# Deformable convolution, attention and experts on one core: all eight chunks of batch 0 transposed on TensorE, and a gate on the finishing chains

## The chip, the core and the metric

The program runs on one core of a Trainium2 chip. The metric is the device time of one execution in microseconds (us), as a median over runs. The five engines each work through their own instruction list in the order in which the program wrote it: TensorE (PE; PEld is its weight load), VectorE (DVE), ScalarE (ACT), GpSimd (POOL) and SyncE (SP). SP here only issues transfers; an issue that waits holds up the issues written behind it.

## The reference, cut to what matters

The input is 4 images of 128 channels by 64 x 64 positions. Per image:

```python
x = x + deform_conv(group_norm(x))       # 3x3 taps: bilinear samples at learned offsets, times a mask,
                                         # then out[o, p] = sum over c, k of samples[c, k, p] * w[o, c, k]
t = to_tokens(x)                         # 4096 tokens of 128 features, 16 heads of 8
t = t + attn(ln(t))                      # q = k = v = ring of cosines; softmax(q q' / sqrt 8) q;
                                         # output projection, ln, feed forward (8 -> 512 -> 128), ln
t = t + experts(ln(t))                   # router over 8 experts, the best two weighted
```

Attention runs over all 4096 tokens of an image, so every token needs the keys of all others.

## The kernel before

**Chunks.** An image is cut into 8 chunks of 512 positions. `prepare(b)` makes everything that attention needs of image b: group norm, a table of corner values in DRAM, offsets and weights, and then `deform` and `convolved` chunk by chunk, which end in `features`: queries, keys and values of the chunk, written to DRAM.

**A chunk's sampling.** `deform` handles 12 units a chunk (3 groups of 3 taps, 4 blocks of 128 positions). A unit is three indirect gathers on POOL (line 625), one multiplication by the bilinear weights and two additions on DVE (lines 645, 650, 651). Then the samples must be turned from position-major to channel-major for the convolution. There are two ways:
- In order: TensorE transposes the unit's three 128 x 128 tiles into PSUM (line 662) and DVE copies them (line 665) into `sT`, which stays in SBUF. `sT` has one buffer, so a chunk's first unit waits until the convolution of the chunk before has read it (`summed`).
- By way of DRAM: DVE transposes 32 x 32 blocks (line 686, three instructions a unit), SP writes them to `smd` (line 698, 12 issues a chunk), and `convolved` reads them back into `sT` (line 731, 12 issues a chunk).

Before the change chunks 0 and 1 of image 0 go in order and the other 30 chunks by way of DRAM. `gather` keeps gathers up to four units ahead for the first 36 units of image 0, two units ahead otherwise; for the deeper lead it borrows spare buffers of another tag (`spare`, tag `et`).

`convolved` (line 281 is its helper `by_columns`) multiplies 9 taps, adds bias and residual (line 758), transposes (765) and runs `features`: layer norm, cosines and their products on DVE, one power (396) and one copy (823) on POOL, a transpose (836), and `hiT` and `loT` (838, 839), which SP writes to DRAM. A chunk counts as prepared some planned microseconds after that.

**Attention.** A step is one 128-token slice of keys against one chunk of queries, for the 4 heads of a group. `scores` issues 4 matmuls (1261) and 2 exponentials on ACT of 128 x 1024 elements each (line 1270), `context` 4 matmuls with the values (1281). There are 7400 exponentials in the program. While image 0 is being prepared, the runs are ordered so that they use what is there: exponentials 1 to 32 need chunk 0 alone, up to 128 chunks 0 and 1, up to 208 chunks 0 to 2, up to 512 chunks 0 to 3, up to 576 also chunks 4 and 5; after that all eight are needed. Runs over part of the keys park sums in DRAM (`part`, line 1126) and load them again (line 1456).

**Finishing.** When the four head groups of a chunk are done, `park_context` puts the chunk on the list `done`. Up to two chains `finishing` run: each takes a chunk from the list and runs `finish`, which loads the chunk's data (lines 1086 to 1102), then `attention_out` (transfers, projection 281 into `ao_ps`, layer norm), `feed_forward` (`z_ps`, `h_ps`, `f_ps`, layer norm) and `experts` (router, then eight expert matmul groups into `e_ps`, sums on DVE 1065 to 1075), ending in a transposed copy `y` (line 892) and the store (line 1081).

**What sets the order.** `Beside` is a planner that runs while the program is being written. It keeps planned times, and after each attention step it lets waiting jobs issue pieces of `prepare`, of finishing, and of other side work, within a budget of TensorE time per step. Each `yield need(...)` names the planned cost of a piece and the earliest planned time. `force` issues pieces of `prepare` without regard to the budget when attention has no keys to go on with; `drain` issues everything that is left after the last attention step, job by job. So the order on each engine is fixed when the program is built; on the chip nothing is reordered.

Of the kernel before, what the change touches and what calls it, by code (L numbers as in the profile page):

```python
# [202 lines left out]
def need(pe=0.0, dve=0.0, lat=0.0, hold=False, after=0.0):  # L203

    return pe, dve, lat, hold, after


def ve(n, ops=1):  # L210

    return ops * (0.17 + n / 960.0)
# [6 lines left out]
def tr(n):  # L219

    return 0.13 + 0.115 * n
# [3 lines left out]
def kernel(  # L225
# [47 lines left out]
    def misc(name):  # L273
        if alone:
            return ps_s.tile([P, 2, 512], F32, tag="sc", name=name)[:, 0, :]
        return ps_m.tile([P, 512], F32, tag="misc", name=name)
# [127 lines left out]
    def settle():  # L404

        nc.vector.tensor_reduce(is_hi, pick[:, 0], AX.XY, ALU.add)
        nc.vector.tensor_reduce(is_lo, pick[:, 1], AX.XY, ALU.add)
        nc.vector.tensor_copy(w1_h, w1_4)
        nc.vector.tensor_tensor(w1_4, w1_4, w1_h.bitcast(F32), ALU.subtract)
        nc.vector.tensor_scalar(w1_h, w1_h.bitcast(F32), is_hi, None, ALU.mult)  # L410
        nc.vector.scalar_tensor_tensor(w1_x, w1_4, is_lo, w1_h.bitcast(F32), ALU.mult, ALU.add)
        for _ in cosine(cry, ry_sb, cry_n, cry_r, 0.0):
            pass
# [185 lines left out]
    def deform(b, tab, idx, wt, rest):  # L599
# [7 lines left out]

        def early(n):

            return b == 0 and n < 3 * 12  # L610

        def gather(last):

# [20 lines left out]
        for n, (ch, kg, j) in enumerate(units):  # L634
            progress[b] = 0.1 + 0.9 * n / len(units)
            if b == 0 and n == 36:
                yield need(dve=5.0)
                settle()
            while not ahead:
                yield need(lat=0.5)  # L640
            v, landed = ahead.pop(0)
            v4 = v.rearrange("p k (q c) -> p (k q) c", c=C)
            w12 = wt[:, j, 3 * kg : 3 * kg + 3, :].rearrange("p k q -> p (k q)")
            yield need(dve=ve(1536), after=landed)
            nc.vector.tensor_tensor(v4, v4, w12[:, :, None].to_broadcast([P, 12, C]), ALU.mult)  # L645
            if moved:
                yield need(pe=0.01, dve=ve(384))
                moved.pop()()
            yield need(dve=ve(768) + ve(384))
            nc.vector.tensor_tensor(v[:, :, : 2 * C], v[:, :, : 2 * C], v[:, :, 2 * C :], ALU.add)  # L650
            nc.vector.tensor_tensor(v[:, :, :C], v[:, :, :C], v[:, :, C : 2 * C], ALU.add)  # L651
            if b == 0 and ch < 2:


                if n % 12 == 0:
                    while len(summed) < ch:
                        yield need(lat=0.5)
                    sT = big.tile([P, KK, CH], F32, tag="xs", name=f"sT_first{ch}")
                yield need(pe=tr(3), lat=FREE, hold=True)
                pt = misc(f"sT_ps{j}_{kg}")  # L660
                for k in range(3):
                    nc.tensor.transpose(pt[:, P * k : P * (k + 1)], v[:, k, :C], ident)

                def move(sT=sT, kg=kg, i=j % 4, pt=pt):
                    nc.vector.tensor_copy(
                        sT[:, 3 * kg : 3 * kg + 3, P * i : P * (i + 1)],
                        pt[:, : 3 * P].rearrange("p (k c) -> p k c", c=P),
                    )

                moved.append(move)  # L670
                beside.later(beside.now + 0.8, lambda n=n: gather(n))
                if n % 12 == 11:
                    yield need(pe=0.01, dve=ve(384))
                    moved.pop()()
                    featuring.append(True)
                    beside.add("prepare", convolved(b, ch, sT), 0.5, True)
                    if ch == 0:
                        yield from rest
                continue

            yield need(dve=ve(384))
            if j % 4 == 0:
                beside.flush(sent)
                tr9 = work.tile([P, 4, 4, 4, 32], F32, tag="st", name=f"tr{b}_{ch}_{kg}", bufs=NST)
            for k in range(3):
                nc.vector.transpose(  # L686
                    out=tr9[:, k, :, j % 4, :],
                    in_=v[:, k, :C].rearrange("p (c i) -> p c i", i=32),
                )
            beside.later(beside.dve, lambda n=n: gather(n))  # L690
            if j % 4 < 3:
                continue
            while kg == 0 and len(featuring) > 1:
                yield need(lat=1.0)

            def put(ch=ch, kg=kg, tr9=tr9):
                for o in range(4):
                    nc.sync.dma_start(
                        out=smd[ch % 2][:, 3 * kg : 3 * kg + 3, :, o].rearrange(
                            "i k c n -> i (k c) n"  # L700
                        ),
                        in_=tr9[32 * o : 32 * (o + 1), :3].rearrange("p k c j t -> p (k c) (j t)"),
                    )

            sent = beside.dve
            beside.later(sent, put)
            if kg == 2:

                while len(summed) < ch if b == 0 else featuring:
                    yield need(lat=1.0)  # L710
                featuring.append(True)
                beside.later(
                    beside.dve + 0.1,
                    lambda ch=ch: beside.add("prepare", convolved(b, ch), 0.5, True),
                )
# [163 lines left out]
    def bc4(v):  # L879
        return v[:, None, :].to_broadcast([P, 4, C])  # L880
# [14 lines left out]
    def attention_out(b, ch, r, aT, a4):  # L895


        yield need(dve=ve(512))
        nc.vector.tensor_tensor(r, r, bc4(b_comb), ALU.add)
        yield need(dve=ve(512), lat=0.2)  # L900
        nc.vector.tensor_tensor(aT, aT, a4.rearrange("p i c -> p (i c)"), ALU.mult)
        for i in range(4):
            if i % 2 == 0:
                yield need(pe=2 * MM128, dve=ve(512) if i else 0.0, lat=0.0 if i else FREE, hold=not i)
            if i == 0:
                po = misc(f"ao_ps{b}_{ch}")
            by_columns(
                po[:, C * i : C * (i + 1)], aT[:, P * i : P * (i + 1)], wcomb_sb, True, True
            )
        nc.vector.tensor_tensor(r, r, po.rearrange("p (i c) -> p i c", c=C), ALU.add)  # L910
        m = work.tile([P, 4], F32, tag="ln_m", name=f"m1{b}_{ch}")
        rs = work.tile([P, 4], F32, tag="ln_r", name=f"r1{b}_{ch}")
        yield from layer_norm_stats(r, m, rs, "ln")
        yield need(dve=ve(128, 4))
        normalized(a4, r, m, rs)
        yield need(dve=ve(512, 2), lat=0.2)
        nc.vector.tensor_tensor(a4, a4, bc4(g1), ALU.mult)
        nc.vector.tensor_tensor(a4, a4, bc4(beta1), ALU.add)
# [165 lines left out]
    def finish(b, ch):  # L1084
        x4 = temp2(f"x4_{b}_{ch}")
        nc.sync.dma_start(out=x4, in_=x2d[b][ch])

        rows = atd[b][ch].rearrange("g (h d) n -> (g h) d n", d=32)
        aT = temp2(f"aT{b}_{ch}", (P, CH))
        nc.sync.dma_start(out=aT, in_=rows[:, :HD])  # L1090
        rd = work.tile([P, CH // HD], F32, tag="rd", name=f"rd{b}_{ch}")
        nc.sync.dma_start(out=rd, in_=rows[:, HD].rearrange("h (q n) -> h q n", q=HD))
        r = temp2(f"r{b}_{ch}")
        nc.sync.dma_start(out=r, in_=xtd[b][ch])
        yield need(lat=4.0)
        yield need(dve=0.6, lat=0.1)
        nc.vector.reciprocal(rd, rd)
        yield need(lat=3.5)
        nc.sync.dma_start(out=rdd[b][ch].rearrange("h q n -> (h q) n"), in_=rd)
        yield need(lat=6.0)  # L1100
        a4 = temp2(f"a4_{b}_{ch}")
        nc.sync.dma_start(
            out=a4.rearrange("p i c -> p (i c)"),
            in_=rdd[b][ch].rearrange("h q n -> h (q n)")[:, None, :].to_broadcast([HEADS, HD, CH]),
        )
        yield from attention_out(b, ch, r, aT, a4)
        yield from feed_forward(b, ch, x4, a4)
        yield from experts(b, ch, x4)


    def park_context(b, g, sc, cu):
# [112 lines left out]

    landing = {}
    fetched = {}
    groups, done, active = {}, [], []

    def finishing():

# [125 lines left out]
    for n, (run, t) in enumerate(steps):  # L1356
        b, g, sc = runs[run][:3]
# [50 lines left out]
    n = issued = begun = 0  # L1408
    beside.rate = 1.0
    with tc.manual_schedule(engines={PE, DVE, SP, POOL}):  # L1410
# [6 lines left out]
        while n < len(steps):  # L1417
# [11 lines left out]
            b, g, sc, ts, kind = runs[run]  # L1429
# [145 lines left out]
```

## Time and profile before

| | before |
|---|---|
| median of 11 runs | 7461.85 us (7451.89 to 7480.11) |
| profiled execution: time, span | 7461.57 us, 7459.8 us |
| granted TensorE clock | 0.969 |
| PE busy | 7025.7 us (94%) |
| ACT busy | 6853.4 us (92%), of it 6839.4 in 7400 exponentials |
| DVE busy | 4464.3 us (60%) |
| POOL busy | 1659.7 us (22%) |
| first exponential starts, last ends | 174.0 us, about 7375 us |

The span runs from the first to the last instruction. Matmuls are pipelined, and a busy TensorE is not one at its peak. A group's line gives busy time, mean duration and the idle time of its engine before it with what ended that.

### The profile page before, as it was taken

To read this page: it belongs to the slowest core of one execution; us is meant where nothing else is said; L and a number is where in the kernel's file an instruction comes from. 1 tells how busy PE (TensorE), PEld (TensorE's weight loads), DVE (VectorE), ACT (ScalarE), POOL (GpSimd) and SP (SyncE) were. 2 spreads that over 40 slices of the span, in tenths; PEclk is the share of its full clock that TensorE was granted. 3 is DMA by queue.
4 is the path that set the end of the run, shared out by engine and by line. 5 is a ranking of instruction groups with operands and counts; after the bars stand their busy time and mean duration, and the time that the engine had idled before them with its cause. 6 is when DMAs were issued, how large, how long until landed. Compare 5 with 4: busy or idle time off the path is not lost.

```text
span 7459.8 us, 180754 instructions
## 1 busy us (share of the span) xinstructions
PE 7025.7 (94%) x73848; PEld 2352.9 (32%) x73848; DVE 4464.3 (60%) x8950; ACT 6853.4 (92%) x7467; POOL 1659.7 (22%) x1326
## 2 busy tenths in 40 slices
PE   3689999899999999999999999989999999999997
PEld 2222232223333333333333333323333333333333
DVE  7766366676445777775544778775444554455544
ACT  0579999899999999999999999989999999999995
POOL 5545044443001433431000434430000000000000
PEclk6889999999999999999999999999999999999998
DMA  6777477988446888887555888996454466666651
GB/s 182 225 211 232 132 243 245 306 258 279 146 165 228 292 270 274 280 277 231 201 180 195 266 287 293 313 314 225 172 180 150 158 234 232 237 223 229 233 194 64
DMA packets 909789, 1689.53 MB, mean 226 GB/s; under 512 B 150754, under 2 KB 384124, under 8 KB 858268
## 3 DMA queue, kind: packets, MB, share of 16 engines
q1 hardware_dynamic: 809102, 1371.37, 55.4%
q0 software_dynamic: 92160, 302.06, 12.4%
q8 instruction: 580, 9.50, 0.5%
q10 hardware_dynamic: 7694, 4.52, 0.2%
q14 instruction: 253, 2.07, 0.1%
HBM read 1027.51 MB, written 650.14 MB: 225 GB/s over the span
## 4 chain that ended last, share of the span: by engine, by line
PE 79%; DMA 10%; DVE 4%; issue 1%; SPq 1%; POOL 1%; ACT 1%; POOLq 0%; DVEq 0%; ACTq 0%
PE acc L1281 39%; PE sc L1261 23%; PE acc L1214 5%; PE e_ps L281 4%; PE conv_ps L281 3%; DMA et<-etd 3%; PE f_ps L281 2%; DMA etd<-st 1%; DMA sT<-smd 1%; PE om_ps L533 1%; DMA smd<-tr 1%; DMA v<-tab,idx 1%; DVE v L645 1%; DVE st L1140 1%; ACT e L1270 1%
## 5 line engine op out<-in xcount | busy, mean ns | idle before, releaser
L1270 ACT ACTIVATE e<-sc 128x1024 f32<-128x1024 f32 x7400 | 6839.4, 1084 | 414.9 <-PE sc L1261 331.5
L1281 PE MATMUL acc<-e,qf 128*9 128x512 f32 (+1 forms) x29600 | 3900.8, 599 | 12.1 <-ACT cu L1491 6.4
L1261 PE MATMUL sc<-qT,kT 32*128 32x512 f32 x14800 | 2323.7, 498 | 112.3 <-ACT e L1270 60.8
L1261 PEld LDWEIGHTS sc<-qT,kT 32*128 32x128 f32 x14800 | 925.6, 183 | 3533.8 <-ACT e L1270 3329.9
L625 POOL DMA_INDIRECT v<-tab,idx x1152 | 1459.6, 1267 | 1502.0 <-DVE tr L686 874.1
L1140 DVE STREAM_TRANSPOSE st<-e 128x1024 f32<-128x1024 f32 x792 | 937.4, 1222 | 714.7 <-ACT e L1270 606.1
L1281 PEld LDWEIGHTS acc<-e,qf 128*9 128x9 f32 (+1 forms) x29600 | 677.7, 91 | 580.4 <-issue 316.6
L396 POOL TENSOR_TENSOR r<-ln_t,expo 128x4 f32<-128x4 f32 x96 | 112.2, 1169 | 3097.3 <-DVE ln_t L394 3049.4
L645 DVE TENSOR_TENSOR v<-v,wt 128x1536 f32<-128x1536 f32 x384 | 667.3, 1738 | 129.7 <-DMA v<-tab,idx 128.0
L1214 PE MATMUL acc<-et,qv 128*9 128x128 f32 x12672 | 502.7, 277 | 72.6 <-DMA et<-etd 72.6
L1065 DVE TENSOR_TENSOR eo<-e_ps,gt 128x512 f32<-128x512 f32 x256 | 175.1, 686 | 534.5 <-PE e_ps L281 530.7
L650 DVE TENSOR_TENSOR v<-v 128x768 f32<-128x768 f32 x384 | 367.1, 956 | 10.1
L281 PE MATMUL conv_ps<-sT,wconv_sb 128*32 128x256 f32 x4320 | 348.5, 397 | 11.3 <-DMA sT<-smd 8.9
L1214 PEld LDWEIGHTS acc<-et,qv 128*9 128x9 f32 x12672 | 269.3, 90 | 272.1 <-issue 202.9
L686 DVE STREAM_TRANSPOSE tr<-v 128x128 f32<-128x128 f32 x1080 | 249.5, 282 | 52.0 <-DMA etd<-st 43.3
L1493 DVE COPY cu<-acc 128x512 f32<-128x512 f32 x116 | 80.2, 692 | 282.2 <-PE acc L1281 282.0
L651 DVE TENSOR_TENSOR v<-v 128x384 f32<-128x384 f32 x384 | 215.8, 562 | 13.3
L396 POOL TENSOR_TENSOR rstd<-lt_t,expo 128x4 f32<-128x4 f32 x32 | 56.5, 1766 | 542.0 <-DVE lt_t L394 519.3
L281 PE MATMUL f_ps<-w_sb,h 128*32 128x128 f32 x4096 | 166.5, 283 | 0.0
L950 DVE TENSOR_SCALAR h<-h_ps,b_sb 128x512 f32<-128x512 f32 x128 | 94.9, 743 | 99.5 <-PE h_ps L948 92.0
L823 POOL COPY fx<-rn 128x512 f32<-128x512 f32 x32 | 26.8, 839 | 521.6 <-DVE rn L822 303.2
L965 DVE TENSOR_TENSOR a<-a,f_ps 128x512 f32<-128x512 f32 x32 | 21.9, 685 | 196.2 <-PE f_ps L281 196.2
(227 smaller groups left out, 3164.8 us busy)
## 6 DMA issues: line engine op xcount, KB each, us to landing
etd<-st SPq DMA_DIRECT2D x396, 1024.0 KB
et<-etd SPq DMA_DIRECT2D x396, 1024.0 KB
kT<-kTd SPq DMA_DIRECT2D x372, 256.0 KB
smd<-tr SPq DMA_DIRECT2D x360, 192.0 KB
sT<-smd SPq DMA_DIRECT2D x360, 192.0 KB
qT<-qTd SPq DMA_DIRECT2D x166, 256.0 KB
atd<-cu SPq DMA_DIRECT2D x128, 256.0 KB
qf<-fqd SPq DMA_DIRECT2D x372, 72.0 KB
```

What stands on the lines that cost most here:

```text
L281: nc.tensor.matmul(dst[c : c + 32], lhsT=lhsT[:, c : c + 32], rhs=rhs, start=start, stop=stop)
L625: nc.gpsimd.indirect_dma_start(out=v[:, k, :], out_offset=None, in_=tab, in_offset=bass.IndirectOffsetOnAxis(ap=idx[:, j, kk : kk + 1], ax ...
L645: nc.vector.tensor_tensor(v4, v4, w12[:, :, None].to_broadcast([P, 12, C]), ALU.mult)
L650: nc.vector.tensor_tensor(v[:, :, : 2 * C], v[:, :, : 2 * C], v[:, :, 2 * C :], ALU.add)
L651: nc.vector.tensor_tensor(v[:, :, :C], v[:, :, :C], v[:, :, C : 2 * C], ALU.add)
L686: nc.vector.transpose(out=tr9[:, k, :, j % 4, :], in_=v[:, k, :C].rearrange("p (c i) -> p c i", i=32),)
L1065: nc.vector.tensor_tensor(ws[hf], pe.rearrange("p (e c) -> p e c", c=C), gt[:, i, 4 * hf : 4 * (hf + 1), None].to_broadcast([P, 4, C]), AL ...
L1140: nc.vector.transpose(out=st[:, :, 2 * pr : 2 * pr + 2, :].rearrange("p o h (q j) -> p o (h q) j", j=32), in_=es[pr].rearrange("p h (q o i ...
L1214: nc.tensor.matmul(acc[32 * h : 32 * h + QW, P * kt : P * (kt + 1)], lhsT=qv[:, at : at + QW], rhs=e[:, :, h, 32 * t : 32 * (t + 1)], star ...
L1261: nc.tensor.matmul(ps[i // 2][:, i % 2, :], lhsT=kT[h : h + 32, P * (t % 4) : P * (t % 4 + 1)], rhs=qT[h : h + 32, :], start=True, stop=True,)
L1270: nc.scalar.activation(e, ps[pr], AF.Exp, scale=1.0 / math.sqrt(HD))
L1281: nc.tensor.matmul(acc[32 * h : 32 * h + width, :], lhsT=flat[:, first : first + width], rhs=es[h // 2][:, h % 2, :], start=(t == ts[0]), ...
```

## The change

Three edits:
- `early(n)` holds for all units of image 0, so gathers run up to four units ahead there and two of five units sit in spare buffers.
- In `deform`, all eight chunks of image 0 take the in-order way; the way through `smd` remains for images 1 to 3.
- In `finish`, a list `heavy` is a gate between `attention_out` and `feed_forward`: a chain waits, one planned microsecond at a time, until no other chain is inside `feed_forward` or `experts`. It holds for every chunk of all four images.

```diff
         def early(n):
-            return b == 0 and n < 3 * 12
+            return b == 0
...
-            if b == 0 and ch < 2:
+            if b == 0:
                 if n % 12 == 0:
                     while len(summed) < ch:
                         yield need(lat=0.5)
                     sT = big.tile([P, KK, CH], F32, tag="xs", name=f"sT_first{ch}")
...
         yield from attention_out(b, ch, r, aT, a4)
+        while heavy:
+            yield need(lat=1.0)
+        heavy.append(True)
         yield from feed_forward(b, ch, x4, a4)
         yield from experts(b, ch, x4)
+        heavy.pop()
...
-    groups, done, active = {}, [], []
+    groups, done, active, heavy = {}, [], [], []
```

## The prediction

> **What bounds the kernel now.** I read the head of the page first, then busy time by stretches, then the costliest groups of the long stretch, then the timeline of ScalarE at the beginning and of all engines at the end.
>
> The stretches (us, then busy time of each engine with its count, granted clock, share of the DMA engines, GB/s):
>
> ```profile
> 150.00:600.00 450.00, 321.99 (x2514) 95.14 (x2514) 315.39 (x562) 287.41 (x320) 252.38 (x190) 0.82 0.75 229
> 600.00:850.00 250.00, 248.18 (x2078) 71.52 (x2076) 136.19 (x272) 249.63 (x273) 77.06 (x60) 1.00 0.58 172
> 5150.00:7375.00 2225.00, 2222.20 (x25075) 769.86 (x25076) 1063.06 (x2466) 2222.51 (x2429) 54.24 (x53) 1.00 0.58 199
> 7375.00:7459.80 84.80, 34.69 (x433) 21.17 (x425) 52.08 (x147) 0.23 (x1) 3.02 (x3) 0.64 0.07 23
> ```
>
> From 5150 to 7375 us ScalarE is busy for 2222.5 of 2225 us, and its group there was idle for 2.0 us:
>
> ```profile
> L1270 ACT ACTIVATE e<-sc 128x1024 f32<-128x1024 f32 x2411 | 2223.0, 1081 | 2.0 <-ACT e L1270 0.8 <-PE sc L1261 0.3 <-PE h_ps L948 0.2
> ```
>
> 2223.0 / 2411 = 0.922 us an exponential, back to back. ScalarE is the bound wherever attention has keys: finishing work written beside attention is free there, and taking it away gains nothing. Time is lost where ScalarE idles: before the first exponential (174 us), between first and last (by the stretches: 600 - 174 - 287.4 = 138.6 us up to 600, 0.4 to 850, 26.1 to 1150, 181 in the later preparations, about 350 in all), and after the last (85 us). The change acts on the first 900 us and on the end.
>
> ScalarE early on and around the last wait for keys:
>
> ```profile
> 218.02 0.59 ACT L1491 COPY cu<-acc 128x512 f32<-128x512 f32 x1 [1.22 <-PE acc L1281]
> 266.23 5.61 ACT L1270 ACTIVATE e<-sc 128x1024 f32<-128x1024 f32 x6 [47.62 <-PE sc L1261]
> ...
> 851.25 16.61 ACT L1270 ACTIVATE e<-sc 128x1024 f32<-128x1024 f32 x18 [0.26 <-PE sc L1261]
> 879.85 3.77 ACT L1270 ACTIVATE e<-sc 128x1024 f32<-128x1024 f32 x4 [11.99 <-PE sc L1261]
> ```
>
> 47.6 us wait for chunk 1, which was in order already, and 12.0 us for chunk 7. And the end, one finishing chain alone:
>
> ```profile
> 7375.89 0.69 DVE L1493 COPY cu<-acc 128x512 f32<-128x512 f32 x1
> ...
> 7386.78 0.69 DVE L892 COPY y_6T<-y_ps 128x512 f32<-128x512 f32 x1 [0.57 <-PE y_ps L890]
> 7387.39 0.54 DVE L1097 RECIPROCAL rd<-rd 128x64 f32<-128x64 f32 x1
> ...
> 7399.64 1.12 DVE L788 TENSOR_SCALAR a<-r,m,r 128x128 f32<-128x128 f32 x4 [1.19 <-POOL r L396]
> ...
> 7430.16 0.29 DVE L1007 COPY lT<-l_ps 128x128 f32<-128x128 f32 x1 [0.78 <-PE l_ps L1002]
> ...
> 7455.46 0.69 DVE L892 COPY y_7T<-y_ps 128x512 f32<-128x512 f32 x1 [0.57 <-PE y_ps L890]
> 7456.18 0.34 SPq L1081 DMA_DIRECT2D out_dram<-y_7T  x1
> ```
>
> A whole chain takes 7456.15 - 7387.47 = 68.7 us from one y to the next, every step waiting for the one before; the last store takes 3.65 us more.
>
> **Part 1, the gate: the end.** The order of instructions of both programs is fixed and can be compared. After the last scores, the order before holds the last part of chunk 6's experts and all of chunk 7. The changed order holds six outputs: chunk 2 from its router on (lT), chunks 4, 5, 6, 7 whole, and chunk 3 from the normalisation ahead of its feed forward. The cause is visible in the order: before, two chains alternate; now `z` transposes of successive chunks stand 168 exponentials (168 x 0.922 = 155 us) apart, one chain at a time. In batch 3 this falls behind. On DVE each whole finish stands strictly behind the y of the one before, so chains cannot overlap. Sum from the last context copy (ends 7376.58): chunk 2, 7430.16 to 7456.15, 26.0; four whole, 4 x 68.7 = 274.7; chunk 3, 7399.64 to 7456.15, 56.5; store 3.65. Together 360.9 against 7459.8 - 7376.6 = 83.2 now: **+278**. Attention returns nothing for it, for ScalarE idles 2.5 us in 5150 to 7375. Bounds: -15 if loads of the next chunk hide a little, +25 if each chain pays 5 us more at the lower clock (0.60 in this stretch): 263 to 303.
>
> The chain holds a write and a read back of the reciprocals: issue at 7387.96, read issued at 7389.73, consumer at 7392.93, so 1.8 and 3.2 us. The Trainium skill, "DMA: Bandwidth & Descriptors", in "Anatomy of one DMA — SWDGE (gpsimd) path", gives about 2 us fixed for a DMA, most of it the receipt of the write; these two are issued by SP. By it the two would be some 4 us instead of 5, an estimate, and the four whole chains 4 us shorter; I use the measured chain.
>
> **Part 2, a new wait at exponential 584.** Order before: chunk 7's transpose of `features` (836) stands behind exponential 564, 20 ahead of need. Changed: after exponential 584 stand the last two units' transposes, chunk 7's whole convolution (72 fours of matmuls in a row), line 765 and 836, and only then the next scores. Why so late: outside the opening runs the planner pays TensorE work from a budget, and the transposes (0.475 planned a unit, 5.7 a chunk) now come out of it. Queued behind the wait is all of attention. Chain by rows: multiplication, additions, transposes and copy of the last units about 8 us; convolution 9.8 (chunk 0, 114.2 to 124.0); 2.1 to the end of line 758; 29.5 from there to the end of `loT` (126.1 to 155.6); then 18.4 (chunk 0, 155.6 to 174.0) to 31 us (chunk 7, 849.0 to 879.9) until the next exponential. That is 68 to 81, less 2 for the exponential still running, less the 12 idle now: **+60** (54 to 67).
>
> **Part 3, the rest of the opening.** For chunks 2 to 7 of image 0 the change removes per unit 3 block transposes (3 x 0.282 = 0.85 us DVE) and adds one copy (0.55): 72 x 0.30 = 21 us less DVE. It adds 216 transposes on PE: in the trace 0.272 us in `fT_ps` at a granted clock of 1.00 and a median of 0.421 in `sT_ps` at 0.53 to 0.64, so 59 to 91 us of PE, beside ScalarE from 600 on. They are written between attention's own matmuls, so a late unit now holds attention, which the DVE route could not do. DVE waited 67.1 us for gathered samples from 174 to 900, 28 times; with a lead of four that shrinks, and 2.4 us a time is about what three score tiles hide: I take +15 (0 to 60).
>
> The Trainium skill, "TensorE: Matmul & The Clock Gate", Part 4, says that a transpose does not count as work that lifts the clock. The row above fits, 0.421 in the starved stretch. If all 216 ran so, TensorE would pay 91 us instead of 59, a difference of 32 us, an estimate that lies mostly under waits; the sum above does not use it.
>
> SP loses 24 issues a chunk, 144 in all. This is the gain:
>
> ```profile
> ACT cu L1491 <- PE acc L281: 49.6, 11, 12.0
> ```
>
> ScalarE waited 49.6 us, 11 times, for accumulators whose parked sums come late; in the SP list the load of `part` stood behind the `smd` and `sT` issues (8 of them from 269.4 to 275.8 just ahead of the 12.0 us wait). Between nothing and all 49.6 I take **-35**, as most lie next to such issues, some behind issues that wait for POOL.
>
> The order also moves the starving: chunk 2's features come after exponential 128 instead of 94, all that two chunks allow, so attention waits there; chunk 3's come after 176 instead of 200, against a need at 208, where ScalarE now idles 15.0 and 9.0 us (its timeline, at 482.6 and 499.9). Features of chunk 1 no longer stand behind chunk 2's units on DVE. I set these against each other: 0 (-20 to +25).
>
> **Batches 1 to 3.** 181 us of ScalarE idle time; the changed order holds about as many finishes in those stretches. I take 0, bounds -50 to +25.
>
> **Sum.** 278 + 60 + 15 - 35 + 0 + 0 = +318 on the profiled 7461.57 us (span 7459.8, 1.8 around it; the median of the runs is 7461.85): 7780.
>
> **Rivals.**
> - *POOL becomes the opening's limit.* Its list is in order; with four units ahead up to 2 x 3 x 1.27 = 7.6 us more gathers stand ahead of each power (396) and copy (823). Against: POOL is busy 252 of 450 us. Price: 2 x 7.6 a chunk, five chunks, +76: 7856. Chance 0.08.
> - *The tail overlaps after all.* DVE is busy 41.1 of the 68.7 us of a chain. If chains ran at DVE's pace, 4.8 of them (four, and 56.5 / 68.7) would save 27.6 each, 132: 7648. Against: DVE's own list puts them end to end. Chance 0.05.
> - *Faster: idle time inside attention is what the change returns.* Place: between first and last exponential, 350 us less the 47.6 that stay = 302. If the `smd` traffic and the second chain caused all of it, the wait at 584 included, 7461.6 + 278 - 302 = 7437. It decides only if over 92% of that idle time goes (278 / 302). For it: SP waits for DVE in the preparations. Against: 181 us lie in images that keep `smd`. Chance 0.01.
> - *The gate does nothing*, if chains rarely met: 7462 + 40 = 7502. The order speaks against it. Chance 0.01.
>
> **How the numbers follow.** The forecast has 0.85. Low ends: 263 + 54 + 0 - 50 - 20 - 50 = +197, high ends: 303 + 67 + 60 + 0 + 25 + 25 = +480; not all at once, so I take 7690 to 7870, which includes the POOL case. A difference under 0.2% (15 us) cannot be told from none. Faster 0.01, same 0.01, slower 0.98.
>
> **What would show it.** A stretch after the last exponential near 360 us with DVE about 60% busy and six y copies, four of them 68 to 70 us apart; one gap of ScalarE of 65 to 80 us ahead of exponential 585; waits for `acc L281` well under 49.6. If the tail stays under 150 us, or the last exponential ends before 7375, the prediction is wrong.

## The result and the profile after

The changed kernel takes 7790.6 us, median of 8 runs (7777.0 to 7799.3), against 7463.6 us for the kernel before (31 runs): a ratio of 1.0437 [1.0427, 1.0446], 4.4% slower. The forecast was 7780. The profiled execution has a span of 7790.1 us, 330.3 more than the 7459.8 before.

The stretches of the changed kernel, cut as before (us, then busy time of PE, PEld, DVE, ACT and POOL with counts, granted clock, share of the DMA engines, GB/s; the last two cuts are moved to its own last exponential):

```profile
150.00:600.00 450.00, 366.28 (x2907) 116.45 (x2907) 285.69 (x446) 326.60 (x363) 234.70 (x181) 0.87 0.60 188
600.00:850.00 250.00, 240.12 (x2015) 73.01 (x2014) 132.75 (x205) 228.75 (x248) 82.30 (x67) 0.98 0.43 136
5150.00:7428.00 2278.00, 2274.43 (x24953) 776.78 (x24945) 1020.53 (x2267) 2276.77 (x2490) 47.58 (x47) 1.00 0.59 202
7428.00:7790.10 362.10, 150.91 (x1778) 88.22 (x1778) 223.09 (x672) 4.36 (x10) 16.10 (x16) 0.62 0.06 18
```

Up to 600 us ScalarE does more than before (326.6 us against 287.4), up to 850 less (228.8 against 249.6). The last stretch is the result: 362.1 us with next to no attention in it, where there were 84.8. DVE is busy for 223.1 of them, and the granted clock is 0.62.

The timeline of VectorE in that stretch, at the y copies:

```profile
7457.72 0.69 DVE L892 COPY y_2T<-y_ps 128x512 f32<-128x512 f32 x1 [0.57 <-PE y_ps L890]
7458.33 0.54 DVE L1097 RECIPROCAL rd<-rd 128x64 f32<-128x64 f32 x1
...
7525.85 0.69 DVE L892 COPY y_4T<-y_ps 128x512 f32<-128x512 f32 x1 [0.57 <-PE y_ps L890]
7526.46 0.54 DVE L1097 RECIPROCAL rd<-rd 128x64 f32<-128x64 f32 x1
...
7730.64 0.69 DVE L892 COPY y_7T<-y_ps 128x512 f32<-128x512 f32 x1 [0.57 <-PE y_ps L890]
7731.25 1.11 DVE L788 TENSOR_SCALAR a<-r,m,r 128x128 f32<-128x128 f32 x4
...
7786.15 0.69 DVE L892 COPY y_3T<-y_ps 128x512 f32<-128x512 f32 x1 [0.57 <-PE y_ps L890]
```

Right behind each y copy stands the reciprocal that begins the next chain (or, for chunk 3, line 788 of its second part). The six copies end at 7458.4, 7526.5, 7594.8, 7663.0, 7731.3 and 7786.8 us: chains of 68.1, 68.3, 68.2 and 68.3 us end to end, then a part of 55.5. One chain by itself, as a stretch:

```profile
7458.41:7526.47 68.06, 26.85 (x325) 16.22 (x325) 41.01 (x125) 0.23 (x1) 3.02 (x3) 0.60 0.07 21
```

DVE works 41.0 of 68.1 us and waits for the rest. The rival in which the tail runs at DVE's pace is out.

The timeline of ScalarE at the other place, the new wait ahead of exponential 585:

```profile
819.34 20.45 ACT L1274 ACTIVATE e<-sc 128x1024 f32<-128x1024 f32 x22
884.82 5.61 ACT L1274 ACTIVATE e<-sc 128x1024 f32<-128x1024 f32 x6 [45.04 <-PE sc L1265]
```

It is 45.0 us long, where there were 12.0, and where the prediction's sign was a gap of 65 to 80. The timeline of the other engines within it:

```profile
842.64 7.95 PE L281 MATMUL conv_ps<-sT_first,wconv_sb 128*32 128x256 f32 x144
850.66 1.13 DVE L758 SCALAR_TENSOR_TENSOR xr<-conv_ps,bconv_sb,xr 128x128 f32<-128x128 f32 x4 [8.22 <-PE conv_ps L281]
...
871.79 0.69 DVE L839 TENSOR_TENSOR loT<-fT_ps,hiT 128x512 fp32r<-128x512 f32 x1
...
883.93 1.22 PE L1265 MATMUL sc<-qT,kT 32*128 32x512 f32 x6 [12.90 <-DMA kT<-kTd]
```

The last exponential before it ends at 839.8. Last units 2.8, convolution 8.0, line 758 1.2, features up to `loT` 20.7, then 12.3 for the last keys' way through memory to the next exponential.

And the waits of ScalarE for parked accumulators (174 to 960 us; total us, how often, the longest), which were 49.6, 11 and 12.0:

```profile
ACT cu L1495 <- PE acc L281: 17.5, 10, 6.7
```

Where the 330.3 us are, by the ends of numbered exponentials in the two traces:

| stretch | before | after | difference |
|---|---|---|---|
| end of exponential 584 | 867.9 | 839.8 | -28 |
| idle between 584 and 585 | 12.0 | 45.0 | +33 |
| end of exponential 7400 (the last) | 7374.8 | 7431.0 | +56: -28, +33, and +51 after 585 |
| from there to the end | 85.0 | 359.1 | +274 |

The +51 lies mostly in the preparations: ScalarE idles 69.5 us instead of 52.9 between exponentials 900 and 1700 (image 1 is prepared), 80.5 instead of 41.7 between 2300 and 3400 (image 2), and 92.2 instead of 78.5 between 4000 and 5000 (image 3); the stretches between them idle some 14 us less.

### The profile page after: what moved, and what is told of

Its sections match the earlier page's. It is cut to its first block, busy times and chain, and to the rows that moved or that the text cites. A ratio compares the mean times of both kernels' runs of the same rounds, so it can differ in the third digit from the quotient of the medians.

```text
span 7790.1 us, 180928 instructions
## 1 busy us (share of the span) xinstructions
PE 7158.7 (92%) x74064; PEld 2417.4 (31%) x74064; DVE 4456.0 (57%) x8806; ACT 6850.9 (88%) x7467; POOL 1665.9 (21%) x1326
## 4 chain that ended last, share of the span: by engine, by line
PE 78%; DMA 10%; DVE 6%; issue 3%; SPq 1%; POOL 1%; ACT 1%; ACTq 0%; POOLq 0%; DVEq 0%
PE acc L1285 38%; PE sc L1265 23%; PE acc L1218 5%; DMA et<-etd 4%; PE conv_ps L281 3%; PE e_ps L281 3%; PE f_ps L281 2%; DMA sT<-smd 2%; PE om_ps L533 1%; DMA etd<-st 1%; ACT e L1274 1%; PE sT_ps L662 1%; PE ao_ps L281 1%; DVE v L645 1%; POOL v L625 0%
## 5 line engine op out<-in xcount | busy, mean ns | idle before, releaser
L1265 PE MATMUL sc<-qT,kT 32*128 32x512 f32 x14800 | 2360.7, 498 | 52.2 <-ACT e L1274 32.9
L1265 PEld LDWEIGHTS sc<-qT,kT 32*128 32x128 f32 x14800 | 947.3, 183 | 3496.9 <-ACT e L1274 3317.2
L281 PE MATMUL conv_ps<-sT,wconv_sb 128*32 128x256 f32 x3456 | 283.0, 400 | 54.2 <-DMA sT<-smd 51.4
L686 DVE STREAM_TRANSPOSE tr<-v 128x128 f32<-128x128 f32 x864 | 199.2, 281 | 17.5 <-DMA etd<-st 10.9
L662 PE MATMUL sT_ps<-ident,v 128*128 128x128 f32 x288 | 63.6, 340 | 130.0 <-issue 108.5
```

Of the source, the lines that this page charges most:

```text
L281: nc.tensor.matmul(dst[c : c + 32], lhsT=lhsT[:, c : c + 32], rhs=rhs, start=start, stop=stop)
L686: nc.vector.transpose(out=tr9[:, k, :, j % 4, :], in_=v[:, k, :C].rearrange("p (c i) -> p c i", i=32),)
L1265: nc.tensor.matmul(ps[i // 2][:, i % 2, :], lhsT=kT[h : h + 32, P * (t % 4) : P * (t % 4 + 1)], rhs=qT[h : h + 32, :], start=True, stop=True,)
```

## The experiments

The tail is the time from the end of the last exponential to the end of the program. The theory: the gate (`heavy`) makes the tail, and the in-order transposes make the wait ahead of exponential 585. The first rival: the longer tail comes from the whole change of order, the gate being harmless. The second: the in-order transposes cost the opening more than they return. Three sets ran, each on another chip, on which the kernel before took 7607.55, 7579.99 and 7462.70 us; so ratios are compared, and traces within a set, or of the third set with the traces shown so far, whose kernel before took the same time (7463.6).

**The gate alone.** The kernel before, with the gate around feed forward and experts, and nothing else of the change.

> The kernel before with the gate alone; sampling as before. Theory G (the gate makes the tail; the in-order chunks make the loss of about 51 us between exponentials 585 and 7400): the order holds the end of chunk 2, four whole chains, and chunk 3 from its feed forward on behind the last scores, so the tail is about 340 us (360.9 less some 20 for chunk 2, which is further on), the last exponential ends near 7375 as before, and the time is about 7715. Theory H (the gate also disturbs attention): the same tail, but the last exponential near 7425 and about 7765. If the tail belongs to the in-order chunks instead: 7462.

Measured: 7937.87 against 7607.55, 1.0433 [1.0406, 1.0461]. The timeline of ScalarE at the end (line 1017 is the exponential of the router, one a chain):

```profile
7589.06 9.31 ACT L1274 ACTIVATE e<-sc 128x1024 f32<-128x1024 f32 x10
7650.63 0.23 ACT L1017 ACTIVATE ex<-lg 128x32 f32<-128x32 f32 x1 [52.27 <-DVE lg L1016]
7718.50 0.23 ACT L1017 ACTIVATE ex<-lg 128x32 f32<-128x32 f32 x1 [67.64 <-DVE lg L1016]
7786.62 0.23 ACT L1017 ACTIVATE ex<-lg 128x32 f32<-128x32 f32 x1 [67.89 <-DVE lg L1016]
7854.59 0.23 ACT L1017 ACTIVATE ex<-lg 128x32 f32<-128x32 f32 x1 [67.75 <-DVE lg L1016]
7906.84 0.23 ACT L1017 ACTIVATE ex<-lg 128x32 f32<-128x32 f32 x1 [52.02 <-DVE lg L1016]
```

Five chains pass their router behind the last exponential, four of them 67.9 to 68.1 us apart (the idle time, plus 0.23); the tail has 336.5 us. The gate by itself has the ratio of the whole change, but not all of it is tail: without any gate the tails of these runs are 80.5 to 85.0 us, so some 250 of the 330 us are tail and some 80 lie ahead of it, an estimate, for there is no trace of the kernel before on this chip. The two theories on record gave 0 and about 50 there.

**The change without the gate.** Two-chain finishing again; it uses 12 `f2` buffers instead of 11.

```diff
-NF2 = 11
+NF2 = 12
-        while heavy:
-            yield need(lat=1.0)
-        heavy.append(True)
...
-        heavy.pop()
```

> All eight chunks of image 0 in order with gathers four ahead, without the gate, and one more buffer of the finishing tag (12 for 11). Theory G: tail as before (83 us from the last context copy), exponential 585 ends near 886, and the 51 us stay: last exponential near 7431, time about 7516. Theory H: the 51 us go with the gate: last exponential near 7380, about 7465. The wait at exponential 584 (45 us of ScalarE) is there under both.

Measured: 7640.98 against 7607.55, 1.0048 [1.0030, 1.0066], the tail 83.3 us, the wait ahead of exponential 585 44.8 us. The in-order part costs half a per cent and has the wait; the tail is the gate's. The ratio lies between those of the two theories (7516 and 7465 against 7462, 1.007 and 1.000), and the parts do not simply add up: 1.0433 and 1.0048 alone, and 1.0437 for the whole change in the first runs.

**The gate in some images only.** With the gate off in image 3 (first edit), the backlog could only come from images 0 to 2; with the gate on in image 3 alone (second edit, 12 buffers), only from image 3.

```diff
-        while heavy:
+        while heavy and b < NB - 1:
```

> The changed kernel with the gate for images 0 to 2 only. If the chains fall behind in image 3, as the prediction says, the tail shrinks to the 85 us of before and the time to about 7515. If they fall behind earlier and image 3 cannot catch up, four whole chains and two parts stay behind the last scores (its order holds y of 3, 4, 5, 6, 7 and 2 there): tail about 305 us, time about 7735.

```diff
-        while heavy:
+        while heavy and b == NB - 1:
```

> The changed kernel with the gate for image 3 only (and 12 finishing buffers). If the backlog is made in images 0 to 2, this has only the end of chunk 5, a whole chain 7 and chunk 6 from its feed forward behind the last scores: tail about 145 us, time about 7575 with the last exponential near 7431. If image 3 alone made it, the tail would be near 360 us and the time near 7790.

One run each: 7893.35 (1.0376) with a tail of 307.6 us, and 7692.32 (1.0111) with one of 134.4. The timeline of ScalarE at the end of the second, with the gate in image 3 alone:

```profile
7539.47 16.69 ACT L1274 ACTIVATE e<-sc 128x1024 f32<-128x1024 f32 x18
...
7609.10 0.23 ACT L1017 ACTIVATE ex<-lg 128x32 f32<-128x32 f32 x1 [52.94 <-DVE lg L1016]
7662.88 0.23 ACT L1017 ACTIVATE ex<-lg 128x32 f32<-128x32 f32 x1 [53.55 <-DVE lg L1016]
```

Two chains pass their router after the last exponential there, not five. Beyond the 83.3 us without any gate, images 0 to 2 make 224 us of the tail and image 3 makes 51. The y copies show how the one gets into the other. With the gate in images 0 to 2 those of image 2 leave mostly 154 to 155 us apart, the last at 7317.8 us, 266 us before attention ends, where it leaves at 6676.7 without a gate in these images; what is left of image 3 then goes 68 us apart (7601.5, 7669.4, 7737.6, 7805.9, 7874.1), although image 3 has no gate there. So beside attention a gated chain takes 154 us, too long to catch up; after attention chains stand end to end with or without a gate. The changed kernel has the same picture: its y copies are 154.5 us apart from 6603.6 to 7221.5, and the last one of image 2 leaves at 7067.0 (6496.3 before).

These four runs also show the gate in the preparation of image 2. The stretch from exponential 2300 to 3400, the gate alone and then the change without the gate:

```profile
2619.00:3744.00 1125.00, 1064.37 (x11047) 351.98 (x11043) 738.91 (x1440) 1019.30 (x1104) 303.98 (x247) 0.97 0.76 247
```

```profile
2646.50:3731.80 1085.30, 1053.22 (x11136) 350.61 (x11132) 742.45 (x1479) 1018.73 (x1105) 306.82 (x244) 0.99 0.78 253
```

The same work of ScalarE (1019 us) takes 1125 and 1085 us. Its idle time there is 105.7 us with the gate alone and 108.1 with the gate in images 0 to 2, 66.6 without it and 76.4 with the gate in image 3 alone. The order shows a difference in the same place: the eight chunk features of image 2 stand within 856 to 864 exponentials in the two gated programs, and within 1050 in the two that have no gate there. That the denser preparation is what costs the 30 to 40 us is argued, not shown. Between exponentials 4000 and 5000 (image 3 is prepared) the gate alone idles 144.9 us and the other three 112.1 to 115.7; this was not taken apart.

**The 12th buffer by itself.** The kernel before with 12 `f2` buffers; every engine's list is the same as with 11.

> The kernel before with 12 finishing buffers for 11; its order on every engine is that of before. A control on the chip of this set: within 0.3% of before, the ScalarE idle time from exponential 585 to 7400 that of before on this chip, tail near 85 us.

One run: 7578.67 against 7579.99. The buffer is worth nothing, and the runs with 12 can be compared with before.

**Only the lead of four.** Gathers of image 0 up to four units ahead, in order only for chunks 0 and 1, no gate.

```diff
-            if b == 0:
+            if b == 0 and ch < 2:
```

> Only the gathers change: four units ahead for all of image 0, chunks 2 to 7 by way of DRAM as before, no gate, 12 finishing buffers. Theory (the lead is what makes the opening faster, the in-order way is what makes chunk 7 late): the waits at 208 and 584 (16 and 12 us in before) vanish, the order has chunk 7's features behind exponential 480, and the ratio is about 0.996. Rival (POOL holds back powers and copies by the longer list of gathers): idle time up to 584 not under that of before, ratio 1.00 or more.

Measured: 7599.99 against 7579.99, 1.0026 [1.0016, 1.0036]. The waits of GpSimd for a free sample buffer (174 to 900 us), with the lead alone:

```profile
POOL v L625 <- DVE tr L686: 78.4, 4, 27.7
```

and in the kernel before with 12 buffers, on the same chip:

```profile
POOL v L625 <- DVE tr L686: 50.1, 12, 10.9
```

The gathers run ahead until they wait for the DVE's transposes in four long stops. ScalarE's idle time from exponential 33 to 128 is 52.8 us against 25.9, and from 129 to 208 42.3 against 13.7; the wait ahead of 585 is gone (0.0 against 11.5). Early attention pays more than the last wait returns: exponential 585 ends at 921.5 us against 907.6, so the rival on record holds, and the theory's 0.996 is missed. Why early attention waits longer was not taken apart.

**Only the in-order transposes.** All eight chunks in order, the lead of four only for the opening units as before, no gate, 12 buffers.

```diff
-            return b == 0
+            return b == 0 and n < 3 * 12
```

> All eight chunks in order, gathers two units ahead from chunk 3 on, no gate, 12 finishing buffers. Theory: the lead hides the gather's latency behind DVE work; without it the order has to wait at 208 (18 forced pieces) and longer at 584 (chunk 6 is late as well), 50 to 65 us more than with four ahead: about 1.012 of before. If the lead is worth nothing, 1.005.

Measured: 7632.82 against 7579.99, 1.0063 [1.0042, 1.0084]; the wait ahead of 585 is 59.2 us. With the lead of four this wait was 44.8 and the ratio 1.0048: the wait comes from the in-order pieces, and the lead shortens it rather than causing it. The expected 1.012 is missed: the two ratios differ by less than their intervals, so in the whole time the lead is worth nothing that these runs can tell.

**More pieces a step.** The prediction put the late transposes of chunk 7 down to the planner's budget. The planner has a second limit, one piece of TensorE side work per attention step. The change without the gate, with up to three pieces a step until chunk 7 of image 0 is prepared:

```diff
-            beside.fills = 3 if run < 12 else 1
+            beside.fills = 3 if run < 12 or (b == 0 and (0, NCH - 1) not in prepared) else 1
```

This lifts both limits, for `step` looks at the budget (`credit`) only where `fills` is 1:

```python
                if job is None or (
                    fills and self.fills == 1 and self.credit - job["need"][0] < -self.LATE
                ):
                    break
```

> All eight chunks in order, no gate, 12 finishing buffers, and the planner may issue three pieces of TensorE side work after a step, not one, until chunk 7 is prepared. Theory: the wait at exponential 584 comes from the limit of one piece a step (12 transposes more a chunk), so chunk 7's transpose now stands behind exponential 544, the 45 us of ScalarE idle time there fall under 5, and the time is about 45 us (0.6%) under the same kernel with one piece a step, which was 1.0048 of before: 0.999 of before. Rival (POOL or DVE is the limit in chunks 4 to 7): the idle time only moves into the steps between 209 and 584, and the ratio stays near 1.005.

Measured: 7541.42 against 7579.99, 0.9939 [0.9918, 0.9959], under the 0.999 of the theory. In the second run of it, below, the ScalarE timeline at exponential 585 is

```profile
818.88 17.68 ACT L1270 ACTIVATE e<-sc 128x1024 f32<-128x1024 f32 x19
836.79 55.41 ACT L1270 ACTIVATE e<-sc 128x1024 f32<-128x1024 f32 x59 [0.24 <-PE sc L1261]
```

The run of 59 begins ahead of exponential 585 and goes through it: the wait is gone. That one piece a step made it, as the theory has it, does not follow, since the budget went with it. The written order tells the two apart. With the budget alone lifted until chunk 7 is prepared, the list of every engine is the same as without the edit, and chunk 7's transpose (836) stands behind exponential 584. With three pieces and the budget kept, chunk 7's convolution begins behind exponential 554 and ends behind 584, and its transpose still stands behind 584. With both lifted, it stands behind 544. So both limits hold the transposes back; what each is worth in time no run shows.

**The same edit on the kernel before, and again on the change without the gate.**

> The kernel before (two chunks in order, 11 buffers, no gate) with three pieces of TensorE side work a step until chunk 7 is prepared. Theory (the budget edit pays only together with the in-order way, whose transposes are what one piece a step holds back): the waits at 208 and 584 (15 and 12 us of ScalarE) go at most, ratio 0.996 to 1.000. Rival (one piece a step was the loss all along): 0.994, the same as with all eight in order.

> The same kernel as nogate_fills, with more rounds and on the chip of this set: 0.9939 again within 0.002, and under fills_before if the in-order way is worth something of its own. The idle time of ScalarE up to exponential 585 is near 131 us, against 174 before.

Measured, both against 7462.70: 7462.59, 1.0000 [0.9991, 1.0009], and 7417.34, 0.9942 [0.9928, 0.9955]. Waits of ScalarE for parked accumulators, first the kernel before with the edit, then the change without the gate with it:

```profile
ACT cu L1491 <- PE acc L281: 46.9, 10, 11.1
```

```profile
ACT cu L1491 <- PE acc L281: 10.0, 9, 2.2
```

On the kernel before the edit takes the idle times ahead of exponentials 209 and 585 away (16.2 to 0.0 us, 12.0 to 1.6), but exponential 585 ends at 881.1 us instead of 880.9: the time went into other waits of the opening (33.6 to 50.2 us from 209 to 584), and the 46.9 us stay. In-order transposes with the lead of four cost half a per cent, the edit alone is worth nothing, and together they are 0.6% faster than the kernel before. No run has the edit with the lead of four and without the in-order way, so which of the two pays with it is not separated. Where, by ScalarE (us):

| | before | after | without gate, three pieces |
|---|---|---|---|
| end of exponential 585 | 880.9 | 885.8 | 845.3 |
| idle, 900 to 1700 | 52.9 | 69.5 | 90.8 |
| idle, 2300 to 3400 | 41.7 | 80.5 | 20.2 |
| idle, 4000 to 5000 | 78.5 | 92.2 | 47.4 |
| idle, 5000 to 7400 | 2.2 | 0.8 | 17.3 |
| end of the last exponential | 7374.8 | 7431.0 | 7329.5 |
| tail | 85.0 | 359.1 | 80.5 |

Of the 45.3 us gained up to the last exponential, 35.6 are there by exponential 585. The later stretches go both ways (+38, -22, -31, +15); none of these was taken apart.

**A smaller gate.** The gate around feed forward alone, experts outside it:

```diff
         yield from feed_forward(b, ch, x4, a4)
-        yield from experts(b, ch, x4)
         heavy.pop()
+        yield from experts(b, ch, x4)
```

> The changed kernel with the gate around feed_forward alone, experts outside. Theory (a chain is about 155 us long under the gate because everything from feed_forward to the store is inside; the shorter the gated part, the less backlog): behind the last scores stand the end of chunk 6, chunk 7 whole and the end of chunk 5, tail about 100 us instead of 359, the wait at 584 still there, ratio 1.005 to 1.012. If any gate makes the backlog: tail above 250 us and 1.03 or more.

Measured: 7521.16 against 7462.70, 1.0085 [1.0069, 1.0100]; the tail is 100.0 us. The wait ahead of 585 is still there:

```profile
877.19 5.60 ACT L1274 ACTIVATE e<-sc 128x1024 f32<-128x1024 f32 x6 [44.56 <-PE sc L1265]
```

From exponential 2300 to 3400 ScalarE idles 20.5 us, against 80.5 with the full gate. With the experts outside the gate all but 15 of the 274 us goes.

## Why the prediction was right, step by step

- **The end** (forecast +278, measured +274). The parts: first 26.0 against 25.5, chains 68.7 against 68.1 to 68.3, last 56.5 against 55.5. Six outputs after the last score, read from the order, were six in the trace. Two experiments carry the cause: the gate alone has a tail of 336.5 us, the change without it 83.3. What was wrong is "In batch 3 this falls behind": the backlog comes mostly from images 0 to 2, and image 3 inherits it.
- **The wait at exponential 584** (forecast +60, bounds 54 to 67; measured +33, outside them). It was there, of the form described, and its terms were too long: last units 8 against 2.8, line 758 2.1 against 1.2, convolution 9.8 against 8.0, features 29.5 against 20.7, the last hop 18.4 to 31 against 12.3. The features' row was the poorest choice: it came from chunk 0, whose features lie among chunk 1's units on DVE, while chunk 7 has no units behind it. The cause was half of it. Part 2 put it down to the budget; by the written order the budget lifted alone moves nothing, and the limit of one piece a step has to go with it.
- **The rest of the opening** (forecast -20 up to exponential 584, measured -28). Parked sums: -35 forecast, -32 measured. Waits for keys, set at 0: in the traces 48.8 to 31.9 us at exponential 33, 0 to 19.9 at 129 and 16.2 to 0 at 209, -13 together. Late units, set at +15, are not seen apart; the first exponential ends 3 us later.
- **Images 1 to 3** (forecast 0, bounds -50 to +25; measured +51). This term failed. "The changed order holds about as many finishes in those stretches" was a count, and did not look at how close the preparation stood: some 39 us are in the preparation of image 2, where the first set shows more idle time with the gate than without, 17 in that of image 1 and 14 in that of image 3, with some 14 us of idle time less elsewhere after exponential 585. In the first set that stretch of image 1 has 76.4 us with the gate alone and 90.6 to 99.9 in the three kernels with in-order chunks, so those 17 seem to go with the in-order part; but the kernel before with three pieces a step, which has two chunks in order, has 71.3 there as well, so their cause stays open.

The total came within 11 us by luck, because misses cancel: 33 - 60 = -27 at exponential 584, 51 - 0 = +51 later, and -8 and -4 elsewhere, +12 in all. What was foreseen with its mechanism is the tail, which is 274 of the 330 us.

GpSimd did not become the limit of the opening. Its waits for the operand of the power (396), in the changed kernel from 174 to 960 us:

```profile
POOL rstd L396 <- DVE lt_t L394: 194.5, 7, 40.8
```

In chunks 1 to 7 it stood idle ahead of each power and began it as soon as VectorE had the operand; no gathers stood in the way. The rival in which idle time returns over 278 us is out: 28 came back.

## What to carry to other kernels

Before a change that keeps units of work apart, read from the written order what is left after the last instruction of the bounding engine, and price it by the whole chain, waits included: here a gate that was to cost nothing beside attention left four chains of 68 us, and parts of two more, for the time after it. Look for its backlog in the earlier stages, for the last one may only inherit it. And where a change hands side work to a planner, look at all of the planner's limits: here, with the limit of one piece a step raised and the budget lifted, the in-order transposes without the gate went from 1.005 to 0.994 of the time before, which is the best kernel of this study.

## What the hardware showed beside that

- The kernel before took 7462.7, 7580.0 and 7607.6 us on three chips. An exponential took 0.922 us in the first trace and in that of the second set (the kernel with 12 buffers). Most of the 117 us between these two traces is ScalarE's idle time: 280.5 us between exponentials 585 and 7400 in the second set against 198.3 in the first, and 173.6 against 151.2 up to 585. From exponential 5000 on, with image 3 prepared, both idle some 2 us. Why the preparations differ was not tried.
- A 128x128 transpose of fp32 through TensorE, in the tile `sT_ps` of the changed kernel (least, median and largest ns of one):

```profile
L662 PE MATMUL sT_ps<-ident,v x288: 272/328/477, 61.8 to 841.6; 128*128 128x128 f32 x144
```

The fastest take 272 ns; the median over the opening is 328, where 421 had been read from the two opening chunks alone. The Trainium skill, "TensorE: Matmul & The Clock Gate", Part 4, says that transposes do not count as work that lifts the clock. No run here tests this: the stretch with the most of them (150 to 600 us) has a granted clock of 0.87, above the 0.82 before, but it also holds more attention.
